# Handing the first tokens of the second layer over inside SBUF, with its weights loaded a stage earlier

## The chip, the cores and the metric

The kernel runs on one core of a Trainium2 chip. The metric is the device time of one execution in microseconds (us); the time given for a kernel is the median of its runs. The profile is one execution recorded by the hardware profiler, and all rows and lines quoted come from it. PE is the matrix engine, DVE the vector engine, ACT the scalar engine, POOL the general engine (GpSimd), and SP the engine that here only issues transfers (DMAs).

## The reference, cut to what matters

128 images of 128x128 pixels are turned into 64 tokens of 256 features each, by two convolutions. Two transformer layers follow.

```
h = tokenizer(x)                                    # (128, 64, 256)
h = h + relu_attention(layernorm(h))                # layer 0, within an image
h = h + expert_attention(layernorm(h))              # layer 0, 4 experts, residual inside
h = h + linear_attention(layernorm(h))              # layer 1, over the IMAGES, per token group
h = h + experts(layernorm(h))                       # layer 1, 8 experts, each token to one
```

What matters here is the border between the third and the fourth line. The attention of layer 0 works within one image, so its kernel keeps images on the partitions in pairs: partition `b*64 + t` holds token t of image b of the pair, and there are 64 pairs. The attention of layer 1 mixes over the 128 images for each token position, so it wants one image per partition, and tokens along the free axis. Between the two, h has to be turned round.

## The kernel before

All of h lives in SBUF as one tile, `c.h2`, [128, 64 pairs, 256], through the tokenizer and layer 0. Each stage is written in a hand-made order (`tc.manual_schedule()`): the order in the program is the order on each engine's queue, and only the semaphores that the framework derives from the data add waits.

**Expert attention** (`expert_attention`, L770 to L1318) loops over pairs p = 0 to 63. Iteration p works on three pairs at once: `new` (p+1: queries, keys, values), `cur` (p: scores, softmax) and `old` (p-1: transposed weights, `mixed`, `output`). The softmax of a pair comes in two halves x = 0 and 1: `less_max` on DVE (L1078, L1079), `exponents` on ACT (L1082), `sums` on DVE (L1085, L1086), `weights` on POOL (L1092, L1093: the gate into the reciprocal sums, then a product over 128x1024), `transposed` on PE with a copy by ACT (L1102, L1105). `mixed` (L1115, copy L1123) and `output` (L1129) end with `h2[:, p] += po` on DVE (L1130). In the last iteration, p = 63, there is no `new`, and after the loop pair 63 goes through `transposed`, `mixed` and `output` alone. After every fourth pair `output` writes four pairs, 512 KB, to a DRAM tensor `hd` of [image, token, feature] (L1132, on SP). This DRAM copy is what turns h round.

**Linear attention** (`linear_attention`, L1321 to L1788) works on 16 groups of four tokens. `Group.load` (L1370) reads hd[:, 4 tokens, :] (512 KB) into one of four buffers `x`; `statistics` on DVE (L1378, L1379, two instructions per token); `factors` on POOL (L1383 to L1386, four instructions per group); `normal` on ACT (L1389, one per token); `transpose` by PE with a copy by ACT (L1398, L1399). Then `queries_keys(i)` for each token (PE, L1426: four 128x512 matmul instructions each) with `queries_keys_kept` (DVE, L1430), `values` and so on, for four blocks of heads. Other steps are put at places of this loop by `at(n, i, step)`: block n, token i. The matmul results of `queries_keys` and `values` share a ring of three PSUM buffers (`psp`).

At the border everything is done in this order: pair 63 is added, the last four pairs are written to hd, the memory of h2 is released, new pools are opened, `Routing` loads a bias and a gate weight (SP) and makes its constants (POOL, one small PE product `wsum`, L1817), the weights `w`, `wvs`, `bs`, `bvs`, `wgs` are loaded on ACT's queue (L1340 to L1352), the groups 0 to 3 are loaded on SP's queue, and the statistics of groups 0, 1 and 2 begin:

```
            for g in range(4):
                groups[g].load()
            for g in range(3):
                for i in range(NG):
                    groups[g].statistics(i)
                groups[g].factors()
                if g == 0:
                    for i in range(NG):
                        groups[0].normal(i)
                    groups[0].transpose()
            groups[4].load()
```

`c.busy(out, x, n)` (L47) issues n matmuls of the identity with `x` whose result nobody reads.

Of the kernel before, what the change touches and what calls it, by code (L numbers as in the profile page):

```python
# [20 lines left out]
P = 128  # L21
B = 128
# [268 lines left out]
class Shared:  # L291
# [3 lines left out]
    def __init__(self, c, ctx):  # L295
        def pool(name, bufs, **k):
            return ctx.enter_context(c.tc.tile_pool(name=name, bufs=bufs, **k))

        self.np_, self.bp = pool("an", 2), pool("ab", 2)
        self.atp, self.ep, self.small = pool("aat", 1), pool("ae", 2), pool("as", 1)  # L300
        self.psq = pool("apq", 4, space=PSUM)
# [468 lines left out]
def expert_attention(c, sh, hd, normw, wr, br, wqkv, wvT, wproj, bproj, wout):  # L770
# [227 lines left out]
    class Pair:  # L998
# [89 lines left out]
        def weights(self, x):  # L1088

            e, sm = self.e[x], self.sm[x]  # L1090
            s2 = sm.rearrange("p (m e) -> p m e", e=2)
            nc.gpsimd.tensor_mul(s2, s2, bcast(self.blk.gate[:, self.n, x::2], 1, 8))  # L1092
            nc.gpsimd.tensor_mul(e, e, bcast(sm, 2, T))  # L1093
# [31 lines left out]
        def output(self):  # L1125
            p = self.p
            po = ps([P, D], "po")
            for fc in range(2):
                nc.tensor.matmul(po, self.z[:, fc], wt.o[:, fc, :], start=(fc == 0), stop=(fc == 1))  # L1129
            nc.vector.tensor_add(h2[:, p], h2[:, p], po)  # L1130
            if p % 4 == 3:
                nc.sync.dma_start(  # L1132
                    hd[2 * p - 6 : 2 * p + 2].rearrange("(n b) t f -> (b t) n f", b=2),
                    h2[:, p - 3 : p + 1],
                )

# [33 lines left out]
    def do(key):  # L1170
        for step in work.pop(key, ()):
            step()
# [46 lines left out]
    def first(cur, new, chunk, last):  # L1219

        new.queries_keys(0)
        chunk.exponents()
        new.queries_keys_copied(0)
        chunk.sums()
        chunk.weights()
        cur.scores()
        cur.less_max(0)
        y.normal_scalar(0)
        new.queries_keys(1)
        cur.less_max(1)  # L1230
        chunk.transpose()
        new.queries_keys_copied(1)
        chunk.transposed()
        cur.exponents(0)
        last.outcome(0)
        last.outcome(1)
        for par in range(2):
            last.outcome_copied(0, par)
        cur.sums(0)
        cur.weights(0)  # L1240
        cur.exponents(1)
        for par in range(2):
# [12 lines left out]
        new.values_kept(1)  # L1255
        last.back(2)
        last.back(3)
        last.added(2)
        last.added(3)
        for k in range(NB):  # L1260
            x.stream(k)
        do((0, "POOL"))
        do((0, "PE"))

    def rest(chunk, last):
        with (
# [6 lines left out]
            for p in range(NP):  # L1273
                new = Pair(p + 1, blocks[(p + 1) // NB]) if p + 1 < NP else None
                if p == 0:
                    first(cur, new, chunk, last)
                    old, cur = cur, new
                    continue
                do((p, "ACT"))
# [12 lines left out]
                cur.exponents(0)  # L1292
                if new:
                    new.queries_keys(1)
                    new.queries_keys_copied(1)
# [25 lines left out]
def linear_attention(c, hd, hx, out, k, wqk, bqk, wv, bv, wgb):  # L1321
# [7 lines left out]
    NG = 4  # L1329
    with (  # L1330
        tc.tile_pool(name="lw", bufs=1) as wp,
# [7 lines left out]
        w = wp.tile([P, 2, 2 * D], F32, name="w")  # L1339
        nc.scalar.dma_start(w, wqk.rearrange("(c p) n -> p c n", p=P))  # L1340
        wvs = wp.tile([P, 2, D], F32, name="wvs")
        nc.scalar.dma_start(wvs, wv.rearrange("(c p) n -> p c n", p=P))
        bs = wp.tile([P, 2 * D], F32, name="bs")
        nc.scalar.dma_start(bs, bqk.partition_broadcast(P))
        bvs = wp.tile([P, 32], F32, name="bvs")
        nc.scalar.dma_start(bvs, bv)

        wgs = wp.tile([P, 4, 32], F32, name="wgs")
        nc.gpsimd.memset(wgs, 0.0)
        for j in range(2):  # L1350
            r = slice(j * 64, j * 64 + 64)
            nc.scalar.dma_start(wgs[r, :, j * E : j * E + E], wgb.rearrange("(p f) e -> f p e", f=64))  # L1352
        ones = wp.tile([P, P], F32, name="ones")
        nc.gpsimd.memset(ones, 1.0)

        share = wp.tile([P, P], F32, name="share")
        nc.gpsimd.memset(share, 0.0)
        for hh in range(2):
            nc.gpsimd.memset(share[hh * 64 : hh * 64 + 64, hh * 64 : hh * 64 + 64], 1.0 / 64)

        class Group:
# [5 lines left out]
            def load(self):  # L1367
                g = self.g
                self.x = gp.tile([P, NG, D], F32, tag="x", name="x", bufs=4)
                nc.sync.dma_start(self.x, hd[:, g * NG : g * NG + NG, :])  # L1370

            def statistics(self, j):
                if j == 0:
                    self.mv = gp.tile([P, NG, 2], F32, tag="mv", name="mv", bufs=4)
                    self.rs = gp.tile([P, NG], F32, tag="rs", name="rs", bufs=4)
                    self.nb = gp.tile([P, NG], F32, tag="nb", name="nb", bufs=4)
                st = gp.tile([P, 6], F32, tag="st", name="st")
                nc.vector.bn_stats(st, self.x[:, j, :])  # L1378
                nc.vector.bn_aggr(self.mv[:, j, :], st)  # L1379

            def factors(self):
                mean, var = self.mv[:, :, 0], self.mv[:, :, 1]
                nc.gpsimd.tensor_scalar_add(self.rs, var, LN_EPS)  # L1383
                nc.gpsimd.tensor_tensor(self.rs, self.rs, c.nhalf[:, 0:NG], ALU.pow)
                nc.gpsimd.tensor_mul(self.nb, mean, self.rs)
                nc.gpsimd.tensor_sub(self.nb, c.zero[:, 0:NG], self.nb)  # L1386
# [250 lines left out]
        for n, x in enumerate(heads[:3]):  # L1637
# [52 lines left out]
        def last():  # L1690
# [55 lines left out]
            t = gp.tile([P, NG, D], F32, tag="x", name="dev", bufs=4)  # L1746
            routing.statistics(t, gp.tile([P, NG, D], F32, tag="x", name="var", bufs=4))
# [22 lines left out]
        with tc.manual_schedule():  # L1770
            for g in range(4):
                groups[g].load()
            for g in range(3):
                for i in range(NG):
                    groups[g].statistics(i)
                groups[g].factors()
                if g == 0:
                    for i in range(NG):
                        groups[0].normal(i)
                    groups[0].transpose()  # L1780
            groups[4].load()
            for n, x in enumerate(heads):
# [15 lines left out]
class Routing:  # L1798


    def __init__(self, c, gp, wg, bg):
# [5 lines left out]
        self.bgs = gp.tile([P, E], F32, name="bgs")  # L1807
        nc.sync.dma_start(self.bgs, bg.partition_broadcast(P))
        wgs = gp.tile([P, 2, E], F32, name="wgs")
        nc.sync.dma_start(wgs, wg.rearrange("(c p) e -> p c e", p=P))  # L1810
        self.ones = gp.tile([P, P], F32, name="ones")
        nc.gpsimd.memset(self.ones, 1.0)
        self.wsum = gp.tile([P, E], F32, name="wsum")
        with c.tc.tile_pool(name="gw", bufs=1, space=PSUM) as gpp:
            pw = gpp.tile([P, E], F32, name="pw")
            for fc in range(2):
                nc.tensor.matmul(pw, self.ones, wgs[:, fc, :], start=(fc == 0), stop=(fc == 1))  # L1817
            nc.vector.tensor_copy(self.wsum, pw)
# [13 lines left out]
        self.before = gp.tile([P, P], F32, name="before")  # L1832
# [4 lines left out]
        self.one = gp.tile([P, T], F32, name="one")  # L1837
        nc.vector.memset(self.one, 1.0)
        self.c = c
        self.mean, self.rs = (gp.tile([P, T], F32, name=n) for n in ("mean", "rs"))  # L1840
# [329 lines left out]
def vit_tower(ctx: ExitStack, tc: tile.TileContext, a, out):  # L2170
# [8 lines left out]
    with tc.tile_pool(name="stream", bufs=1) as sp:  # L2179
        c.h2 = sp.tile([P, B // 2, D], F32, name="h2")  # L2180
        tokenizer(c, a["x"], a["w1"], a["bn1"], a["w2"], a["bn2"])
        with ExitStack() as rings:
            sh = Shared(c, rings)
            beside, rest = expert_attention(
                c, sh, hd, *(a[k] for k in ("normw", "wr", "br", "wqkvf", "wvf", "wproj", "bproj", "wout"))
# [3 lines left out]
    with tc.tile_pool(name="gate", bufs=1) as gp:  # L2189
        k = Routing(c, gp, a["wg"], a["bg"])  # L2190
        linear_attention(c, hd, hx, out, k, a["wqk1"], a["bqk1"], a["wv1"], a["bv1"], a["wg"])
# [72 lines left out]
```

## Time and profile before

| | |
|---|---|
| time, median of 3 runs | 2685.99 us (2681.73 to 2687.66) |
| the profiled execution: time, span | 2687.57 us, 2685.8 us |
| mean granted TensorE clock | 0.981 |
| PE, DVE, ACT, POOL busy | 95%, 75%, 60%, 60% of the span |
| expert attention from 1108 us on, to 1883.4 us | PE busy 744.6 of 775.4 us |
| the border, 1883.4 to 1902.2 us | PE busy 3.6 of 18.8 us |
| linear attention, 1902.2 to 2202 us | PE busy 280.4 of 299.8 us |

How to read it: busy shares over the span mix stages with different limits, so the table's lower rows give the three stretches that the change touches. "Window" rows give, for a stretch of time, the busy time of PE, its weight loads, DVE, ACT and POOL with the number of instructions in brackets, then the mean clock granted to PE (1.00 is full speed, 0.50 half), the busy share of the DMA engines and GB/s. A "chain" row gives start, duration and what the end of the program was waiting for at that moment. A "timeline" row gives start and duration, engine, line, operation, output and inputs, and in brackets how long the engine stood idle before it and for whom.

### The profile page before, as it was taken

To read this page: it belongs to the slowest core of one execution; us is meant where nothing else is said; L and a number is where in the kernel's file an instruction comes from. 1 tells how busy PE (TensorE), PEld (TensorE's weight loads), DVE (VectorE), ACT (ScalarE), POOL (GpSimd) and SP (SyncE) were. 2 spreads that over 40 slices of the span, in tenths; PEclk is the share of its full clock that TensorE was granted. 3 is DMA by queue.
4 is the path that set the end of the run, shared out by engine and by line. 5 is a ranking of instruction groups with operands and counts; after the bars stand their busy time and mean duration, and the time that the engine had idled before them with its cause. 6 is when DMAs were issued, how large, how long until landed. Compare 5 with 4: busy or idle time off the path is not lost.

```text
span 2685.8 us, 80910 instructions
## 1 busy us (share of the span) xinstructions
PE 2539.0 (95%) x35229; PEld 1724.6 (64%) x35229; DVE 2024.2 (75%) x3028; ACT 1624.6 (60%) x3421; POOL 1618.6 (60%) x1381
## 2 busy tenths in 40 slices
PE   8989999999999999899999999999799987999997
PEld 4553444444444444688888888888466565888886
DVE  5759999999999989878877888877367786444443
ACT  2228888888888988766666666665245533332332
POOL 3318889888898998566666666653232312445544
PEclk9999999999999999999999999999899998999998
DMA  3100000000000000000000000000435454555554
GB/s 111 32 13 1 2 2 2 1 2 1 2 2 1 2 12 2 3 12 19 11 11 19 12 19 12 11 19 11 118 64 126 95 123 151 177 193 191 197 186 134
DMA packets 138271, 141.14 MB, mean 53 GB/s; under 512 B 107875, under 2 KB 121701, under 8 KB 130224
## 3 DMA queue, kind: packets, MB, share of 16 engines
q1 hardware_dynamic: 127536, 118.40, 14.8%
q0 software_dynamic: 7648, 14.77, 1.7%
q8 instruction: 278, 4.55, 0.7%
q10 hardware_dynamic: 2720, 2.69, 0.3%
q14 instruction: 89, 0.73, 0.1%
HBM read 104.03 MB, written 32.54 MB: 51 GB/s over the span
## 4 chain that ended last, share of the span: by engine, by line
PE 71%; DVE 18%; issue 4%; ACT 4%; POOL 1%; DMA 1%; DVEq 0%; POOLq 0%; SPq 0%; ACTq 0%
PE sc L340 12%; PE po L2108 6%; DVE m L530 6%; PE ph L2092 6%; PE pc L184 5%; PE pt L1102 4%; PE pqk L1019 4%; PE sc L1066 4%; PE pq L1426 4%; PE pv L1041 3%; PE pz L1115 3%; PE pt L587 2%; PE sc L525 2%; PE pv L1440 2%; PE pk L409 2%
## 5 line engine op out<-in xcount | busy, mean ns | idle before, releaser
L538 POOL TENSOR_TENSOR m<-q,k 128x1024 f32<-128x1024 f32 x384 | 720.1, 1906 | 69.3 <-PE sc L340 56.3
L530 DVE TENSOR_TENSOR m<-pc,k 128x2048 f32<-128x2048 f32 (+1 forms) x320 | 647.2, 2058 | 0.5 <-ACT q L474 0.5
L340 PE MATMUL sc<-m,wide 128*32 128x512 f32 x4096 | 517.3, 598 | 13.9 <-DVE m L530 7.9
L539 ACT ACTIVATE m<-m 128x1024 f32<-128x1024 f32 x384 | 403.0, 1050 | 11.1 <-POOL m L538 10.5
L340 PEld LDWEIGHTS sc<-m,wide 128*32 128x32 f32 x4096 | 127.8, 109 | 281.4 <-issue 165.7
L548 ACT ACTIVATE m<-k,q 128x64 f32<-128x64 f32 x1024 | 271.0, 340 | 0.9 <-DVE k L421 0.9
L1078 DVE TENSOR_REDUCE mx<-sc 128x16 f32<-128x1024 f32 x128 | 156.1, 1220 | 135.3 <-PE sc L1066 135.3
L1093 POOL TENSOR_TENSOR e<-e,mx 128x1024 f32<-128x1024 f32 x128 | 243.6, 1903 | 10.0
L1025 ACT COPY kr<-pqk 128x512 f32<-128x512 f32 x254 | 137.7, 603 | 140.4 <-PE pqk L1019 140.4
L2092 PE MATMUL ph<-xt,w1s 128*128 128x256 f32 x896 | 198.9, 380 | 3.6 <-DVE xt L2083 2.7
L2108 PE MATMUL po<-w2s,hT 128*128 128x256 f32 x896 | 198.0, 379 | 0.0
L1092 POOL TENSOR_TENSOR mx<-mx,gate 128x16 f32<-128x16 f32 x128 | 27.7, 216 | 278.9 <-ACT z L1123 152.7
L2092 PEld LDWEIGHTS ph<-xt,w1s 128*128 128x128 f32 x896 | 169.8, 190 | 28.3 <-DVE xt L2083 3.3
L2108 PEld LDWEIGHTS po<-w2s,hT 128*128 128x128 f32 x896 | 168.1, 190 | 21.7
L1105 ACT COPY pT<-pt 128x512 f32<-128x512 f32 x256 | 139.0, 598 | 50.4 <-PE pt L1102 50.0
L1079 DVE TENSOR_TENSOR e<-sc,mx 128x1024 f32<-128x1024 f32 x128 | 156.7, 1225 | 4.4
L2126 POOL DMA_INDIRECT out<-y,rout x56 | 56.8, 1013 | 167.7 <-ACT hT L2096 124.8
L1085 DVE TENSOR_REDUCE mx<-e 128x16 f32<-128x1024 f32 x128 | 152.5, 1191 | 4.0 <-ACT e L1082 3.8
L1102 PE MATMUL pt<-ident,e 128*128 128x128 f32 x1024 | 143.1, 282 | 9.5 <-DVE vr L1055 6.3
L2096 ACT ACTIVATE hT<-ph,w1s 128x256 f32<-128x256 f32 x224 | 93.2, 471 | 96.8 <-PE ph L2092 96.8
L2113 ACT ACTIVATE y<-y,gf 128x256 f32<-128x256 f32 x56 | 28.0, 507 | 196.4 <-issue 107.3
L1082 ACT ACTIVATE e<-e 128x1024 f32<-128x1024 f32 x128 | 139.5, 1090 | 2.2 <-DVE e L1079 1.9
(330 smaller groups left out, 5013.6 us busy)
## 6 DMA issues: line engine op xcount, KB each, us to landing
w1s<-in_we SPq DMA_DIRECT2D x30, 1028.0 KB, 5.2
w2s<-in_we SPq DMA_DIRECT2D x30, 1024.0 KB, 4.9
hd<-h SPq DMA_DIRECT2D x16, 512.0 KB, 3.4
x<-hd SPq DMA_DIRECT2D x16, 512.0 KB, 3.9
h<-hd SPq DMA_DIRECT2D x4, 2048.0 KB, 12.8
hx<-h SPq DMA_DIRECT2D x4, 2048.0 KB, 11.8
out<-h SPq DMA_DIRECT2D x4, 2048.0 KB, 20.6
xt<-in_x SPq DMA_DIRECT2D x15, 512.0 KB, 3.6
```

The source lines that it names most:

```text
L340: nc.tensor.matmul(dst[j : j + 32], wide[:, hf, s : s + 32], part, start=start, stop=stop)
L530: nc.vector.tensor_tensor(m, bcast(self.pq[:, hf, i : i + n], 3, T), k, ALU.max)
L538: nc.gpsimd.tensor_tensor(m, bcast(self.q[:, hf, s : s + 2], 3, T), k, ALU.subtract)
L539: nc.scalar.activation(m, m, AF.Relu)
L548: nc.scalar.activation(self.parts[i, hf][:, q], self.blk.k[:, hf, i], AF.Relu, bias=self.q[:, hf, i - NB // 2, q : q + 1], scale=-1.0,)
L1078: nc.vector.tensor_reduce(mx, sc, AX.X, ALU.max)
L1079: nc.vector.tensor_sub(e, sc, bcast(mx, 2, T))
L1085: nc.vector.tensor_reduce(self.sm[x], self.e[x], AX.X, ALU.add)
L1093: nc.gpsimd.tensor_mul(e, e, bcast(sm, 2, T))
L1102: nc.tensor.transpose(pt[:, cq, :], e[:, i : i + 2, :].rearrange("p e s -> p (e s)"), c.ident)
L2092: nc.tensor.matmul(ph[:, j], self.w1[:, w0 : w0 + P], self.xt[:, fc], start=(fc == 0), stop=(fc == 1))
L2108: nc.tensor.matmul(po, self.hT[:, f, r * P : r * P + P], self.w2[:, f, :], start=(f == 0), stop=(f == 7))
```

## The change

The second layer's weights and the first 16 tokens of every image (groups 0 to 3) are put into SBUF during the expert attention. For that, the tiles of the ReLU attention that are free after pair 0 are allocated on the other side of SBUF and released early, and a new class `Front` allocates there. At pair 8 it issues the weights' loads on SP and five memsets on POOL. At every fourth pair from p = 7 on it loads the rows of the eight images that were written four pairs earlier: 8 partitions of 16 KB. Pairs 60 and 61, pair 62 and pair 63 are written to hd on their own. Images 120 to 125 follow after pair 62; images 126 and 127 (pair 63) are copied from h2 to `x` within SBUF, one transfer for each image, before pair 63's write to hd.

In the last iteration `mixed` and `output` of pair 62 move up to just after `exponents(0)` of pair 63, three idle matmuls follow, and `weights(1)` of pair 63 goes to DVE. At the start of the linear attention seven idle matmuls are issued, the four group loads are gone, and group 0's factors and normalisation are done in two halves. Routing's loads move behind the load of group 4, its constants to block 0, token 9, and `wsum` to token 10.

```diff
     def output(self):
             nc.vector.tensor_add(h2[:, p], h2[:, p], po)
-            if p % 4 == 3:
+            if p == NP - 1:
+                front.rows(B - 2, B)
+            n = {NP - 3: 2, NP - 2: 1, NP - 1: 1}.get(p, 4 * (p % 4 == 3))
+            if n:
                 nc.sync.dma_start(
-                    hd[2 * p - 6 : 2 * p + 2].rearrange("(n b) t f -> (b t) n f", b=2),
-                    h2[:, p - 3 : p + 1],
+                    hd[2 * (p - n + 1) : 2 * p + 2].rearrange("(n b) t f -> (b t) n f", b=2),
+                    h2[:, p - n + 1 : p + 1],
                 )
+            if p == NP - 3:
+                front.rows(B - 16, B - 8)
+            elif p == NP - 2:
+                front.rows(B - 8, B - 2)
+            elif n == 4 and p > 3:
+                front.rows(2 * p - 14, 2 * p - 6)
...
+        sh.end.close()
+        front.open()
...
+                if p == 8:
+                    front.weights()
...
                 cur.exponents(0)
+                if not new:
+                    old.mixed()
+                    old.output()
+                    c.busy(ps([P, 2 * D], "idle"), wt.w, 3)
                 if new:
                     new.queries_keys(1)
                     new.queries_keys_copied(1)
                 cur.exponents(1)
...
-                cur.weights(1)
+                cur.weights(1, nc.gpsimd if new else nc.vector)
                 do((p, "POOL"))
-                old.mixed()
                 if new:
+                    old.mixed()
                     for h in range(2):
                         new.values(h)
                         new.values_kept(h)
-                old.output()
+                    old.output()
...
+class Front:
+    NG = 4
+    def open(self):
+        pool = self.c.tc.tile_pool
+        self.wp = self.ctx.enter_context(pool(name="lw", bufs=1, side="right"))
+        self.np_ = self.ctx.enter_context(pool(name="ln", bufs=4, side="right"))
+        self.x = self.wp.tile([P, 4, self.NG, D], F32, name="x")
+    def weights(self):
+        self.w = wp.tile([P, 2, 2 * D], F32, name="w")
+        nc.sync.dma_start(self.w, wqk.rearrange("(c p) n -> p c n", p=P))
...
+        self.wgs = wp.tile([P, 4, 32], F32, name="wgs")
+        nc.gpsimd.memset(self.wgs, 0.0)
...
+    def group(self, g):
+        return self.x[:, g % 4]
+    def rows(self, b0, b1):
+        n = 4 * NG
+        x = self.x.rearrange("p g t f -> p (g t) f")
+        if b1 < B:
+            nc.sync.dma_start(x[b0:b1], self.hd[b0:b1, 0:n, :])
+            return
+        for b in range(2):
+            nc.sync.dma_start(x[b0 + b : b0 + b + 1], self.c.h2[b * T : b * T + n, B // 2 - 1, :])
...
             def load(self):
-                self.x = gp.tile([P, NG, D], F32, tag="x", name="x", bufs=4)
+                self.x = front.group(g)
                 nc.sync.dma_start(self.x, hd[:, g * NG : g * NG + NG, :])
...
+        at(0, 9, routing.constants)
+        at(0, 10, lambda: routing.weights_sum(psp.tile([P, 2 * D], F32, tag="pp", name="pw")[:, 0:E]))
...
+            c.busy(psp.tile([P, 2 * D], F32, tag="pp", name="idle"), w[:, 0], 7)
             for g in range(4):
-                groups[g].load()
+                groups[g].x = front.group(g)
             for g in range(3):
                 for i in range(NG):
                     groups[g].statistics(i)
-                groups[g].factors()
+                    if g == 0 and i % 2:
+                        groups[0].factors(i - 1, i + 1)
+                        for j in range(i - 1, i + 1):
+                            groups[0].normal(j)
                 if g == 0:
-                    for i in range(NG):
-                        groups[0].normal(i)
                     groups[0].transpose()
+                else:
+                    groups[g].factors()
             groups[4].load()
+            routing.load()
```

More of the change, by code (lines that the diff above doesn't have):

```diff
@@ L291, with __init__, pool @@
 class Shared:
-    def __init__(self, c, ctx):
-        def pool(name, bufs, **k):
+    def __init__(self, c, ctx, end):
+        def pool(name, bufs, ctx=ctx, **k):
             return ctx.enter_context(c.tc.tile_pool(name=name, bufs=bufs, **k))
-        self.np_, self.bp = pool("an", 2), pool("ab", 2)
-        self.atp, self.ep, self.small = pool("aat", 1), pool("ae", 2), pool("as", 1)
+        self.np_, self.bp, self.small = pool("an", 2), pool("ab", 2), pool("as", 1)
+        self.atp, self.ep = (pool(n, k, end, side="right") for n, k in (("aat", 1), ("ae", 2)))
+        self.end = end
         self.psq = pool("apq", 4, space=PSUM)
@@ L767, in relu_attention, with expert_attention @@
     return old, blocks[-1]
-def expert_attention(c, sh, hd, normw, wr, br, wqkv, wvT, wproj, bproj, wout):
+def expert_attention(c, sh, front, hd, normw, wr, br, wqkv, wvT, wproj, bproj, wout):
     tc, nc, h2 = c.tc, c.nc, c.h2
@@ L1086, in sums, with weights @@
             nc.vector.reciprocal(self.sm[x], self.sm[x])
-        def weights(self, x):
+        def weights(self, x, eng=nc.gpsimd):
             e, sm = self.e[x], self.sm[x]
             s2 = sm.rearrange("p (m e) -> p m e", e=2)
-            nc.gpsimd.tensor_mul(s2, s2, bcast(self.blk.gate[:, self.n, x::2], 1, 8))
-            nc.gpsimd.tensor_mul(e, e, bcast(sm, 2, T))
+            eng.tensor_mul(s2, s2, bcast(self.blk.gate[:, self.n, x::2], 1, 8))
+            eng.tensor_mul(e, e, bcast(sm, 2, T))
         def transposed(self, x):
@@ L1318, in expert_attention, with __init__ @@
     return beside, rest
-def linear_attention(c, hd, hx, out, k, wqk, bqk, wv, bv, wgb):
+class Front:
+    NG = 4
+    def __init__(self, c, hd, wqk, bqk, wv, bv, wgb):
+        self.c, self.hd, self.inputs = c, hd, (wqk, bqk, wv, bv, wgb)
+        self.ctx = ExitStack()
+    def open(self):
[4 more added lines that the diff above has]
+    def weights(self):
+        c, nc, wp = self.c, self.c.nc, self.wp
+        wqk, bqk, wv, bv, wgb = self.inputs
+        self.w = wp.tile([P, 2, 2 * D], F32, name="w")
+        nc.sync.dma_start(self.w, wqk.rearrange("(c p) n -> p c n", p=P))
+        self.wvs = wp.tile([P, 2, D], F32, name="wvs")
+        nc.sync.dma_start(self.wvs, wv.rearrange("(c p) n -> p c n", p=P))
+        self.bs = wp.tile([P, 2 * D], F32, name="bs")
+        nc.sync.dma_start(self.bs, bqk.partition_broadcast(P))
+        self.bvs = wp.tile([P, 32], F32, name="bvs")
+        nc.sync.dma_start(self.bvs, bv)
+        self.wgs = wp.tile([P, 4, 32], F32, name="wgs")
+        nc.gpsimd.memset(self.wgs, 0.0)
+        for j in range(2):
+            r = slice(j * 64, j * 64 + 64)
+            nc.sync.dma_start(self.wgs[r, :, j * E : j * E + E], wgb.rearrange("(p f) e -> f p e", f=64))
+        self.ones = wp.tile([P, P], F32, name="ones")
+        nc.gpsimd.memset(self.ones, 1.0)
+        self.share = wp.tile([P, P], F32, name="share")
+        nc.gpsimd.memset(self.share, 0.0)
+        for hh in range(2):
+            nc.gpsimd.memset(self.share[hh * 64 : hh * 64 + 64, hh * 64 : hh * 64 + 64], 1.0 / 64)
+    def group(self, g):
+        return self.x[:, g % 4]
+    def rows(self, b0, b1):
+        nc, NG = self.c.nc, self.NG
+        n = 4 * NG
[5 more added lines that the diff above has]
+            nc.sync.dma_start(x[b0 + b : b0 + b + 1], self.c.h2[b * T : b * T + n, B // 2 - 1, :])
@@ L1327, in linear_attention @@
+def linear_attention(c, front, hd, hx, out, k):
     tc, nc = c.tc, c.nc
     lgs, sth, routing = k.lgs, k.sth, k
-    NG = 4
+    NG = front.NG
     with (
-        tc.tile_pool(name="lw", bufs=1) as wp,
         tc.tile_pool(name="lg", bufs=2) as gp,
@@ L1338, in linear_attention @@
     ):
[L1339 to L1359, printed above, removed]
+        w, wvs, bs, bvs, wgs = front.w, front.wvs, front.bs, front.bvs, front.wgs
+        ones, share = front.ones, front.share
         class Group:
@@ L1373, in statistics, with factors @@
                 if j == 0:
[L1374 to L1377, printed above, removed]
+                    self.mv = front.np_.tile([P, NG, 2], F32, tag="mv", name="mv")
+                    self.rs = front.np_.tile([P, NG], F32, tag="rs", name="rs")
+                    self.nb = front.np_.tile([P, NG], F32, tag="nb", name="nb")
+                st = front.np_.tile([P, 6], F32, tag="st", name="st")
                 nc.vector.bn_stats(st, self.x[:, j, :])
                 nc.vector.bn_aggr(self.mv[:, j, :], st)
[L1381 to L1386, printed above, removed]
+            def factors(self, i0=0, i1=NG):
+                i = slice(i0, i1)
+                mean, var, rs, nb = self.mv[:, i, 0], self.mv[:, i, 1], self.rs[:, i], self.nb[:, i]
+                nc.gpsimd.tensor_scalar_add(rs, var, LN_EPS)
+                nc.gpsimd.tensor_tensor(rs, rs, c.nhalf[:, i], ALU.pow)
+                nc.gpsimd.tensor_mul(nb, mean, rs)
+                nc.gpsimd.tensor_sub(nb, c.zero[:, i], nb)
             def normal(self, j):
@@ L1745, in last @@
             y.gates_added(1)
-            t = gp.tile([P, NG, D], F32, tag="x", name="dev", bufs=4)
-            routing.statistics(t, gp.tile([P, NG, D], F32, tag="x", name="var", bufs=4))
+            routing.statistics(front.group(0), front.group(1))
             x.gates(0)
@@ L1807, in __init__, with load, weights_sum, constants @@
         self.bgs = gp.tile([P, E], F32, name="bgs")
-        nc.sync.dma_start(self.bgs, bg.partition_broadcast(P))
-        wgs = gp.tile([P, 2, E], F32, name="wgs")
-        nc.sync.dma_start(wgs, wg.rearrange("(c p) e -> p c e", p=P))
-        self.ones = gp.tile([P, P], F32, name="ones")
-        nc.gpsimd.memset(self.ones, 1.0)
[L1813 to L1818, printed above, removed]
+        self.wgs = gp.tile([P, 2, E], F32, name="wgs")
+        self.ones = gp.tile([P, P], F32, name="ones")
+        self.wsum = gp.tile([P, E], F32, name="wsum")
+        self.before = gp.tile([P, P], F32, name="before")
+        self.one = gp.tile([P, T], F32, name="one")
+        self.c, self.gp, self.inputs = c, gp, (wg, bg)
+        self.mean, self.rs = (gp.tile([P, T], F32, name=n) for n in ("mean", "rs"))
+    def load(self):
+        nc, (wg, bg) = self.c.nc, self.inputs
+        nc.sync.dma_start(self.bgs, bg.partition_broadcast(P))
+        nc.sync.dma_start(self.wgs, wg.rearrange("(c p) e -> p c e", p=P))
+    def weights_sum(self, pw):
+        nc = self.c.nc
+        for fc in range(2):
+            nc.tensor.matmul(pw, self.ones, self.wgs[:, fc, :], start=(fc == 0), stop=(fc == 1))
+        nc.vector.tensor_copy(self.wsum, pw)
+    def constants(self):
+        nc, gp = self.c.nc, self.gp
+        nc.gpsimd.memset(self.ones, 1.0)
         def steps(name, pattern, shape, base=0, rows=0):
@@ L1831, in __init__ @@
         self.token = steps("token", [[1, T]], [P, T], base=1, rows=T)
-        self.before = gp.tile([P, P], F32, name="before")
         nc.gpsimd.memset(self.before, 1.0)
@@ L1836, in __init__ @@
         )
-        self.one = gp.tile([P, T], F32, name="one")
         nc.vector.memset(self.one, 1.0)
-        self.c = c
-        self.mean, self.rs = (gp.tile([P, T], F32, name=n) for n in ("mean", "rs"))
     def statistics(self, t, u):
@@ L2181, in vit_tower @@
         tokenizer(c, a["x"], a["w1"], a["bn1"], a["w2"], a["bn2"])
+        front = Front(c, hd, *(a[k] for k in ("wqk1", "bqk1", "wv1", "bv1", "wg")))
         with ExitStack() as rings:
-            sh = Shared(c, rings)
+            sh = Shared(c, rings, ExitStack())
             beside, rest = expert_attention(
-                c, sh, hd, *(a[k] for k in ("normw", "wr", "br", "wqkvf", "wvf", "wproj", "bproj", "wout"))
+                c, sh, front, hd, *(a[k] for k in ("normw", "wr", "br", "wqkvf", "wvf", "wproj", "bproj", "wout"))
             )
@@ L2190, in vit_tower @@
         k = Routing(c, gp, a["wg"], a["bg"])
-        linear_attention(c, hd, hx, out, k, a["wqk1"], a["bqk1"], a["wv1"], a["bv1"], a["wg"])
+        with front.ctx:
+            linear_attention(c, front, hd, hx, out, k)
         experts(c, hx, gfd, out, a["we1"], a["we2"], a["be2"], lambda: route(c, k, gfd))
```

## The prediction

> **What bounds the kernel now.** I read the page first, then cut the span into stretches with the windows view, then followed the chain of waits and the timeline across the border. Windows:
>
> ```profile
> 1883.40:1902.20 18.80, 3.61 (x13) 2.44 (x13) 6.81 (x28) 2.66 (x5) 6.41 (x23) 0.58 0.58 198
> 1902.20:1910.00 7.80, 7.80 (x19) 3.60 (x19) 3.62 (x9) 2.55 (x5) 0.92 (x5) 0.91 0.22 67
> 1910.00:1947.00 37.00, 36.76 (x139) 23.40 (x138) 15.57 (x39) 14.00 (x27) 6.37 (x15) 1.00 0.49 100
> ```
>
> PE is the limit on both sides of the border (36.8 of 37 us busy just after it) and works 3.6 us in the 18.8 us of the border itself. A microsecond taken from the border is a microsecond of span, since everything later hangs on PE's first `pq`. The chain says what fills it:
>
> ```profile
> 1882.95 0.43 DVE h L1130
> 1883.40 2.89 DMA hd<-h
> ...
> 1887.36 7.15 DMA x<-hd
> 1894.53 0.44 DVE st L1378
> ...
> 1898.88 0.61 ACT x L1389
> ...
> 1902.34 7.63 PE pq L1426 x16
> ```
>
> The last addition ends at 1883.37, the round trip through DRAM delays the first statistics to 1894.53 (11.16 us), and from there to the first `pq` (1902.16 in the timeline) it is 7.63 us. The last iteration of the expert attention, in the timeline:
>
> ```profile
> 1870.81 1.21 DVE L1085 TENSOR_REDUCE mx<-e 128x16 f32<-128x1024 f32 x1
> 1872.35 1.63 PE L1129 MATMUL po<-xTr,z 128*128 128x256 f32 x4 [2.53 <-ACT z L1123]
> 1872.67 1.90 POOL L1093 TENSOR_TENSOR e<-e,mx 128x1024 f32<-128x1024 f32 x1
> ...
> 1874.63 1.97 PE L1102 MATMUL pt<-ident,e 128*128 128x128 f32 x8 [0.65 <-POOL e L1093]
> 1874.83 1.90 POOL L1093 TENSOR_TENSOR e<-e,mx 128x1024 f32<-128x1024 f32 x1
> ```
>
> PE waits for POOL here, and runs slowly: the same 8 transposes take 1.09 us at 1863.36. The clock rows for it:
>
> ```profile
> 1868.00:1871.00 3.00, 1.74 (x52) 1.60 (x52) 2.97 (x4) 1.11 (x3) 0.00 (x0) 1.00 0.00 0
> 1874.00:1877.00 3.00, 2.18 (x9) 1.79 (x10) 0.42 (x1) 0.95 (x2) 2.65 (x3) 0.50 0.00 0
> ```
>
> **The change, part by part.** The sum is made against the profiled execution (span 2685.8, time 2687.57, so 1.8 us outside the span). The median of the runs is 1.6 us below that execution; I carry the difference over to the median.
>
> *Part 1, the round trip.* After the addition, SP issues two copies within SBUF, 0.36 us each by the row of L1132, so the second starts about 0.4 us after the addition. No row shows a copy into one partition. From below: the smallest loads land 1.7 to 1.9 us after issue (the DMA view's list of issues: `wr`, `wproj`, `wvf`). From above: 7.15 us, the crowded loads of the border. The queue is otherwise empty, so I take 2.5, towards the last hd write's 2.89 (512 KB against 16 KB each). First statistics at 0.03 + 0.37 + 2.5 + 0.05 = 2.95 us after the addition instead of 11.16: **-8.2** (-8.8 to -3.6). Gone with it are the loads of groups 0 to 3 and the weights, 198 GB/s in the border's row.
>
> What the moved transfers cost where they go: six loads at pair 8, sixteen row loads and two more hd writes, all on SP. In the expert attention SP has nothing else to issue (its wait for L1130 before the last write was 41.7 us), so an SP that waits blocks nobody until pair 63. The tightest: pair 62's hd write (about 1872) must land (2.9) before the rows of images 120 to 125 are issued (1875), which land by about 1878; the copies of pair 63 come at 1883. Five microseconds of cover; without it, up to 3 us. The pair-63 hd write now lands near 1887, and its first reader, group 4's load, is issued only after group 0's transposes (1892). The DMA engines were busy 0.05 of this stage, so transfers there cost nothing.
>
> [...]
>
> *Part 2, the start of the linear attention.* Statistics of two tokens end 1.17 us after the first starts (1894.53 to 1895.70); POOL starts 0.17 later and its four instructions take 1.92 (1896.93 to 1898.85); the second half follows on POOL: 1.17 + 0.17 + 1.92 + 0.07 + 1.92 = 5.25. Two `normal` end 1.07 later (6.32), then transposes and copy: before, `pq` began 1.21 after the last `normal` on a slow clock; on a fast one about 0.95. Total 7.27 against 7.63: **-0.4** (-0.6 to +0.6). Halving the factors gains only 0.1, since POOL pays its four instructions twice; the statistics of groups 1 and 2 stay behind PE's first 6.9 us of `pq`.
>
> *Part 3, the idle matmuls.* One fp32 128x512 product is two instructions in the trace (`pq` x4 for two products), 0.43 us each in the fast stretches. Seven are 6.0 us: from 1883 to 1889, just before the first `normal` ends (1889.3). Nothing needed is behind them unless PE is slow, when they take 12 us and would hold the transposes back by up to 2.5. What they buy: the first 16 `pq` took 7.81 us, fast ones 6.9: **-0.9** (0 to -0.9).
>
> *Part 4, the last iteration.* PE ends pair 62's `pz` at 1869.8; `z` now goes ahead of `exponents(1)`, so `po` runs 1870.3 to 1871.5 and the addition 1871.5 to 1871.95. On DVE this addition stands ahead of `sums(0)`, which ran at 1870.81: everything behind moves 1.16 us, and POOL's `weights(0)` ends at 1875.7 instead of 1874.57. `sums(1)` and its reciprocal end at 1874.85. Then `weights(1)` on DVE: 0.2 and 1.23 us by like rows, so 1876.3 if DVE is free. Here the trace has a row against it, DVE and POOL each multiplying 128x1024 with both inputs in SBUF:
>
> ```profile
> 2174.89 1.23 DVE L1549 TENSOR_TENSOR qk<-qk,ks 128x1024 f32<-128x1024 f32 x1
> 2175.00 2.88 POOL L1549 TENSOR_TENSOR qk<-qk,ks 128x1024 f32<-128x1024 f32 x1 [5.91 <-DVE ks L1544]
> ```
>
> POOL's usual 1.90 became 2.88: it waited for DVE to end. [...] POOL starts first here, so DVE waits until 1875.73 and ends at 1877.2. [...] PE: half 0 from 1875.8 to 1876.9, half 1 from 1877.25 to 1878.35, last copy 1879.15, `pz` to 1880.9 (52 instructions in 1.74 after such a copy at 1868.08), `z`, `po`, addition to 1883.05, against 1883.37: **-0.3** if the clock holds. The three idle matmuls (2.6 us, 1871.5 to 1874.1) leave a gap of 1.7. If it drops as before, the transposes cost 0.88 each and `pz` 0.5 more: +1.2. Range -0.7 to +1.2.
>
> *Part 5, what moves into covered places.* `wsum` at token 10: four small matmuls with their weight loads, 0.99 slow, about 0.5 fast, in a stretch where PE is full: **+0.5** (0.3 to 1.0, with one more tile in the PSUM ring). Routing's constants (2 us) at token 9 fall into POOL's idle 11 us before L1383: 0. Five memsets at pair 8, 0.9 us on POOL, come when POOL had 0.6 us to spare before L1092: **+0.2** (0 to 0.4).
>
> Sum: -8.2 - 0.4 - 0.9 - 0.3 + 0.5 + 0.2 = **-9.1**. Span 2676.7, median 2685.99 - 9.1 = 2676.9; I write 2677. A measurement of this kernel can tell about 0.2% (5.4 us) from no change.
>
> **The rivals.** *The clock stays low* (0.16). For: a pause of 2.5 us at 1869.8 was enough to halve it, and group 0's transposes come in two clumps 2 us apart. Against: the idle matmuls. Without part 3, part 4 at +1.2 and part 2 at 0: -6.3, 2679.7. *The copies land late* (0.13): one partition takes 16 KB, and both copies end on neighbouring partitions; at 7 us instead of 2.5 the gain is -4.6, 2681.4. Against: 16 KB is 1/32 of what took 7.15. *It doesn't do what it says* (0.03): the first statistics still wait for pair 63's write to hd. That lands 0.8 us after the copies, so -8.3: no separate number. *Slower* (0.04): the four groups' buffers become one tile; if waits covered the whole tile, each of the 11 later loads would hold the next statistics until it lands, 3.9 us, of which PE's ring hides about one token, 1.7: 11 x 2.2 = 24, less 9: +15, 2701. It decides from 0.8 us exposed for each load. Against: h2 is also one tile, written slice by slice beside its hd writes, and L1130 waits for nothing but PE there.
>
> **How the numbers follow.** The forecast has 0.64, 2677. The bounds of parts 1 to 5, the late copies and the scatter of the runs (6 us over three) give 2671 to 2682. Faster by over 0.2% needs 5.4 of the 9.1: nearly all of the forecast, four fifths of the low clock, a third of the late copies: 0.85. Within 0.2%: 0.11. Slower: 0.04.
>
> **What would show it.** Right: no `x<-hd` among the chain's pieces at the border; first L1378 row (new number) some 3 us after the last addition, first `pq` some 10 us after it; the stretch between them at a clock above 0.9; the border 9 us shorter and all later stretches as long as before. [...] Wrong: a DVE wait for `x` inside the linear attention, a PE wait before the transposes on the idle matmuls, or an iteration at pairs 8 to 60 longer than before.

## The result, and the profile after

| | before | changed |
|---|---|---|
| time, median of 6 runs each | 2685.89 us (2681.73 to 2687.66) | 2674.6 us (2671.17 to 2677.69) |
| ratio, 95% interval | | 0.9962 [0.9949, 0.9974] |
| the profiled execution: time, span | 2687.57, 2685.8 us | 2677.69, 2675.9 us |
| the same ratio, a second time (8 and 16 runs) | | 0.9970 [0.9958, 0.9983] |

The change makes the kernel faster by 0.3 to 0.4%, about 11 us in the first comparison and 7 us in the second. Executions of one kernel lie 6 to 10 us apart in these two comparisons, and up to 15 us in the experiments, so single microseconds are read from the profiles, as intervals between two events at the border. The last column is the profile of the changed kernel that was taken in the second comparison; there is one profile of before.

| interval (us) | before | changed | difference | changed, repeat |
|---|---|---|---|---|
| start of pair 63's scores to the end of the last addition ("the last iteration") | 18.99 | 18.19 | -0.80 | 18.65 |
| last addition to the first statistics | 11.16 | 3.02 | -8.14 | 3.02 |
| first statistics to the first `pq` | 7.63 | 6.61 | -1.02 | 6.60 |
| first `pq` to the fourth token kept (start of the fourth L1430, now L1488) | 7.85 | 8.69 | +0.84 | 8.73 |
| sum | 45.63 | 36.51 | -9.12 | 37.00 |

The profile of the changed kernel gives no chain of waits across the border, so the border is read from the timeline (the bracket is how long the engine stood idle, and for whom):

```profile
1881.35 0.42 DVE L1132 TENSOR_TENSOR h<-h,po 128x256 f32<-128x256 f32 x1 [5.36 <-PE po L1131]
1881.80 1.25 SPq L1395 DMA_DIRECT2D x<-h  x2
1881.83 6.28 PE L50 MATMUL idle<-w,ident 128*128 128x512 f32 x14 [0.51 <-DVE h L1132]
1883.09 0.59 SPq L1138 DMA_DIRECT2D hd<-h  x1
...
1884.79 0.43 DVE L1435 BATCH_NORM_STATS2 st<-x 128x6 f32<-128x256 f32 x1 [3.02 <-DMA x<-h]
...
1886.39 0.72 POOL L1442 TENSOR_TENSOR rs<-rs,nhalf 128x2 f32<-128x2 f32 x1
...
1891.40 8.65 PE L1484 MATMUL pq<-w,xT 128*128 128x512 f32 x16 [0.24 <-ACT xT L1457]
```

The last addition ends at 1881.77, the two copies are issued at once, and the first statistics start at 1884.79, released by the copies (`x<-h`), no longer by a load from DRAM. The 14 instructions of the seven idle matmuls fill PE's pause to 1888.1. The windows that answer to the three of before (PE, weight loads, DVE, ACT, POOL busy; clock; DMA share; GB/s):

```profile
1881.77:1891.40 9.63, 8.02 (x23) 3.52 (x23) 6.20 (x26) 2.82 (x6) 4.42 (x13) 0.98 0.05 17
1891.40:1900.05 8.65, 8.65 (x18) 3.90 (x19) 3.96 (x11) 2.40 (x5) 1.87 (x6) 0.82 0.23 62
1900.05:1937.05 37.00, 36.76 (x141) 23.45 (x140) 15.34 (x40) 13.53 (x26) 7.68 (x23) 1.00 0.48 100
```

The border's 18.8 us are 9.63 now, its DMA traffic has gone from 198 to 17 GB/s, and its clock from 0.58 to 0.98. The second row has the surprise: the first 16 `pq` run at a mean clock of 0.82, below the 0.91 of before, and take 8.65 us (before 7.81). From there on PE is as full as it was: 36.76 of 37 us.

### The profile page after: what moved, and what is told of

Its sections match the earlier page's. It is cut to its first block, busy times and chain, and to the rows that moved or that the text cites. A ratio compares the mean times of both kernels' runs of the same rounds, so it can differ in the third digit from the quotient of the medians.

```text
span 2675.9 us, 80960 instructions
## 1 busy us (share of the span) xinstructions
PE 2543.2 (95%) x35249; PEld 1724.9 (64%) x35249; DVE 2026.1 (76%) x3030; ACT 1624.4 (61%) x3421; POOL 1617.8 (60%) x1383
```

## The experiments

All are edits of the changed kernel. But for two single executions their medians lie between 2672 and 2680 us, most with overlapping intervals, so the readings rest on the border's intervals, each from one profile. "Addition to statistics" means from the end of the last addition to the first statistics of group 0.

**Where the 8.1 us come from: groups 0 to 3 loaded from DRAM again, the weights still early.**

```diff
-            if p == NP - 1:
-                front.rows(B - 2, B)
...
-            if p == NP - 3:
-                front.rows(B - 16, B - 8)
...
-                groups[g].x = front.group(g)
+                groups[g].load()
```

> The changed kernel, but no row is loaded early and nothing is passed within SBUF: groups 0 to 3 are loaded from hd at the border again. Weights, idle matmuls, last iteration and Routing's places stay changed. Theory (the round trip was the gain): last addition to first statistics goes from 3.02 us to about 7 to 8 (2.9 for the write to land, about 0.5, 4 for the load), so 4 to 5 us slower than the changed kernel, about 2679. It would be the full 11.2 of before only if the crowding by the weights were not part of it. Rival (the gain is mainly the weights' early load and the last iteration): the interval grows by under 2 us and the time stays within 2 us of 2674.6.

Measured: 2676.56 us, ratio 0.9973 [0.9964, 0.9981]. The timeline:

```profile
1877.51 0.42 DVE L1132 TENSOR_TENSOR h<-h,po 128x256 f32<-128x256 f32 x1 [5.36 <-PE po L1131]
1877.96 0.33 SPq L1136 DMA_DIRECT2D hd<-h  x1
...
1879.72 1.74 SPq L1419 DMA_DIRECT2D x<-hd  x4
...
1883.74 0.43 DVE L1427 BATCH_NORM_STATS2 st<-x 128x6 f32<-128x256 f32 x1 [5.80 <-DMA x<-hd]
```

Addition to statistics is 5.81 us with the whole round trip in place, less than the 7 to 8 expected, where before it was 11.16. So 5.35 of the 8.14 us do not belong to the round trip as such. Piece by piece: the write, now of one pair (128 KB) instead of four, is done after 1.76 us (1877.96 to 1879.72; before 2.89); the load follows at once (before 1.07 later, behind the release of h2's memory and Routing's two loads); and it lands in 4.02 us (before 7.15). That is 1.13 + 1.07 + 3.13 = 5.33.

**The last pair through DRAM, all other images early.**

```diff
-            if p == NP - 1:
-                front.rows(B - 2, B)
...
+            if p == NP - 1:
+                nc.sync.dma_start(
+                    front.x.rearrange("p g t f -> p (g t) f")[B - 2 : B], hd[B - 2 : B, 0 : 4 * front.NG, :]
+                )
```

> The changed kernel, but images 126 and 127 go through hd like all others (one load of two rows after their write has landed) in place of the two copies within SBUF. Theory: last addition to first statistics becomes a write's landing (2.9 us for 512 KB before, some 2 to 2.5 for 128 KB), 0.5 and a small load's landing (about 2): 5 to 5.5 us in place of 3.02, so 2 to 2.5 us slower than the changed kernel, about 2677. Rival (the write to hd lands as soon as a copy, and the wait of the statistics is for that write anyway): no difference, 3 to 3.5 us.

Measured: 2679.07 us, ratio 0.9984 [0.9977, 0.9991].

```profile
1879.11 0.42 DVE L1132 TENSOR_TENSOR h<-h,po 128x256 f32<-128x256 f32 x1 [5.36 <-PE po L1131]
1879.56 0.34 SPq L1136 DMA_DIRECT2D hd<-h  x1
...
1881.28 0.24 SPq L1142 DMA_DIRECT2D x<-hd  x1
...
1883.79 0.43 DVE L1437 BATCH_NORM_STATS2 st<-x 128x6 f32<-128x256 f32 x1 [4.25 <-DMA x<-hd]
```

4.26 us (5 to 5.5 were expected): a write of 1.72 and a load of 2.51. The ladder is now whole: 11.16 (before), 5.81 (nothing heavy around the round trip), 4.26 (only 32 KB on the way back), 3.02 (no DRAM). The copy within SBUF, the most striking part of the change, is worth 1.24 us.

**Do the weights' loads explain the 7.15 us landing?** Four kernels tried to put these loads back to the border on ACT's queue, two with the groups' loads late as well, two with them early. All four have this (and idle matmuls of the identity with itself, since `w` is late), and then differ in where the call stands (ahead of the second layer's code, or, in the last two, inside its hand-made order):

```diff
-                if p == 8:
-                    front.weights()
...
-        nc.sync.dma_start(self.w, wqk.rearrange("(c p) n -> p c n", p=P))
+        nc.scalar.dma_start(self.w, wqk.rearrange("(c p) n -> p c n", p=P))
...
+        front.weights()
```

Both ahead of the order:

> The changed kernel with the groups' loads and the weights' loads both back at the border, the weights on ACT's queue as before (the seven idle matmuls are replaced by 28 of 128 columns, which need no weight). With only the groups at the border, last addition to first statistics had been 5.81 us. Theory (most of the 11.16 us of before was crowding: five weight loads and four group loads at once): the interval returns to about 9 us, 3 more than with the groups alone. Rival (the weights land beside them for nothing): it stays near 5.8 us.

> The changed kernel with the weights' loads alone back at the border on ACT's queue (28 idle matmuls of 128 columns in place of the seven of 512), the rows loaded early. Theory (the weights matter only by crowding the rows; alone they land within 5 to 9 us, before the first pq needs them 9.6 us after the last addition): last addition to first statistics 3.0 to 3.6 us and last addition to first pq within 0.5 us of 9.6. Rival (the weights themselves were what the border waited for): first pq 1.5 us later or more.

Both inside it, one execution each:

> As e5, but with the weights' loads written inside the hand-made order of the linear attention, on ACT's queue, so that they are issued at the border and not when the memory comes free (in e5 they went out at about 1113 us, far ahead). Groups 0 to 3 are loaded at the border too. Theory (crowding): last addition to first statistics 7.5 to 9.5 us, in place of 5.8 with the groups alone; before, the group's load took 7.15 us to land against about 3.9 alone. Rival (the landing of before had another reason, such as SP's two small loads ahead of it): 5.8 to 6.5.

> As e6, but with the weights' loads at the border inside the hand-made order, on ACT's queue; the rows early and the copies within SBUF as changed. Theory: ACT issues them ahead of the last addition, they take about 5 us and are in place before pq (9.6 us after the addition); [...] last addition to first statistics 3.0 to 4.5 us, first pq at most 1.5 us later. Rival (the weights were what mattered): first pq more than 3 us later.

Addition to statistics was 5.82 and 5.85 us with the groups late, 3.02 and 3.02 with them early; the times were 2677.43 (ratio 0.9973 [0.9962, 0.9985]) and 2675.11 us (0.9973 [0.9962, 0.9985]), and 2682.19 and 2684.05 in the single executions. That looks like "the weights don't matter", and it would be a wrong reading. The tile view of the weights says when they were issued, first in the third of these kernels, then in the kernel before:

```profile
L1352 ACTq DMA_DIRECT2D w<-in_wqk x1: 378/378/378, 1110.2 to 1110.2; - x1
...
DMA to landing us min/median/max: 4.0/4.0/4.0
```

```profile
L1340 ACTq DMA_DIRECT2D w<-in_wqk x1: 406/406/406, 1886.4 to 1886.4; - x1
...
DMA to landing us min/median/max: 5.3/5.3/5.3
```

They went out at 1110 us (at 1109 to 1114 in all four), as soon as their memory was free, more than 750 us ahead of the border; before, they had to wait for h2's memory. None of the four tested the crowding. What speaks for it is the traffic while the first group's load was on its way, before and in the first experiment:

```profile
1887.36:1894.51 7.15, 0.99 (x4) 0.93 (x4) 0.17 (x1) 0.00 (x0) 1.12 (x8) 0.50 0.82 281
1879.72:1883.74 4.02, 4.02 (x11) 1.71 (x9) 0.00 (x1) 0.00 (x0) 0.00 (x0) 1.00 0.73 218
```

281 GB/s over 7.15 us are 2.01 MB, 218 over 4.02 are 0.88 MB. The difference, 1.13 MB, is about what the six weight loads of before move (512, 256, 256, 16 and twice 8 KB, 1.08 MB). The weights' own landing times say less: `w` took 5.3 us at the border of before against 4.0 above, and `bs` 7.9 against 4.2, but in the changed kernel, at pair 8, they took 4.8 and 6.0. So that the 3.13 us went to the weights' loads is likely, and no experiment shows it.

**Without the ten idle matmuls.**

```diff
-                    c.busy(ps([P, 2 * D], "idle"), wt.w, 3)
...
-            c.busy(psp.tile([P, 2 * D], F32, tag="pp", name="idle"), w[:, 0], 7)
```

> The changed kernel without its three and seven idle matmuls. Theory (they keep PE's clock up): granted clock falls to 0.5 in the last iteration, its two times 8 transposes take 1.97 us in place of 1.09, last scores to last addition 19.5 us or more in place of 18.2; the first pq after the border take 8 us or more for 16; in all 1.5 to 3 us slower than the changed kernel. Rival (they hold the clock in neither place, as the 8.65 us for the 16 pq in the profile suggests): last scores to last addition within 0.3 us of 18.2 and the time the same.

Measured: 2677.4 us, ratio 0.9977 [0.9968, 0.9987]. The last iteration's interval is 20.20 us instead of 18.19. Its timeline and two windows:

```profile
1874.04 3.67 PE L1104 MATMUL pt<-ident,e 128*128 128x128 f32 x16 [4.21 <-POOL e L1095]
...
1877.64 3.13 PE L1117 MATMUL pz<-pT,vr 128*64 128x64 f32 x64
```

```profile
1871.00:1874.00 3.00, 0.00 (x0) 0.00 (x0) 2.90 (x5) 0.00 (x0) 2.12 (x2) 0.84 0.24 76
1874.00:1877.00 3.00, 2.96 (x14) 2.96 (x15) 1.24 (x2) 1.22 (x3) 0.00 (x0) 0.50 0.00 0
```

PE waits 4.21 us with nothing to do, the clock is halved, and the 16 transposes take 3.67 us where the changed kernel needs twice 1.09. The three idle matmuls there are worth 2.0 us against this profile of the changed kernel, and 1.7 against the mean of eight profiles with its last iteration (below). The seven at the border are worth 0.7 us here: statistics to first `pq` 6.75 against 6.61, and the first 16 `pq` 9.24 us against 8.65.

**The last softmax half on POOL again.**

```diff
-                cur.weights(1, nc.gpsimd if new else nc.vector)
+                cur.weights(1)
```

> The changed kernel with pair 63's weights(1) left on POOL. The DVE product stood 0.7 us behind POOL in the changed kernel (its first, 128x16 one took 0.90 us in place of 0.2). Theory [...]: POOL ends half 1 at 1.90 + 0.3 us after half 0, DVE did at 1.29 after it, so last scores to last addition grows by 0.8 to 0.9 us, to 19.0. Rival (the copies by ACT hide which engine does it): it stays within 0.3 us of 18.2.

Measured: 2677.66 us, ratio 0.9979 [0.9969, 0.9989]; the last iteration takes 20.59 us, 2.4 more than in the changed kernel.

```profile
1873.22 1.09 PE L1104 MATMUL pt<-ident,e 128*128 128x128 f32 x8 [1.63 <-POOL e L1095]
...
1875.38 1.97 PE L1104 MATMUL pt<-ident,e 128*128 128x128 f32 x8 [1.07 <-POOL e L1095]
```

The second half's transposes start 2.16 us after the first's (1.29 in the changed kernel): 0.9 us. The rest is the clock (0.57 from 1875 to 1878 us): PE's pause before them grows from 0.20 to 1.07 us, and the eight instructions that took 1.09 take 1.97. In this profile DVE's help is worth more through the clock than by its own speed; the expectation, 0.8 to 0.9 us, had only the latter.

**The old order of the last iteration altogether.**

```diff
-                if not new:
-                    old.mixed()
-                    old.output()
-                    c.busy(ps([P, 2 * D], "idle"), wt.w, 3)
...
-                cur.weights(1, nc.gpsimd if new else nc.vector)
+                cur.weights(1)
                 do((p, "POOL"))
+                old.mixed()
...
+                old.output()
```

> The changed kernel with the last iteration in the old order: mixed and output of pair 62 at its end, weights(1) on POOL, no three idle matmuls. Theory: last scores to last addition returns to the 18.99 us of before, 0.8 us more than the changed kernel, with a low clock in it. Rival (the reorder gained nothing, since the addition of pair 62 now holds sums(0) back): 18.2 us or less.

Measured: 2675.74 us, ratio 0.9971 [0.9962, 0.998]; the interval is 18.82 us, as before's 18.99. Eight profiles with the change's own last iteration (the changed kernel, its repeat, and the runs with late rows, a late last pair or moved weights) have 18.19 to 18.93, on average 18.5. So the three edits together are worth 0.3 to 0.5 us, but two of them without the third cost 1.4 to 1.8 us more than the old order, in one profile each: the new order makes a pause that the idle matmuls and DVE must fill.

**A better order: the first half's sums ahead of pair 62's addition, and the second copy issued on ACT's queue.**

```diff
                     old.mixed()
+                    cur.sums(0)
                     old.output()
...
-            nc.sync.dma_start(x[b0 + b : b0 + b + 1], ...)
+            (nc.sync, nc.scalar)[b].dma_start(x[b0 + b : b0 + b + 1], ...)
```

> The changed kernel with two orders mended: on DVE sums(0) of pair 63 stands ahead of pair 62's addition, and the copy of image 127 goes on ACT's queue, so that it doesn't wait for SP's first issue (0.63 us each in the profile). Theory: last scores to last addition 0.8 to 1.0 us shorter than 18.19 (17.2 to 17.4), last addition to first statistics 0.4 to 0.6 us shorter than 3.02. Rival (the end of the iteration is set by ACT's copies or PE, and the copies land together anyway): both within 0.2 us of the changed kernel. In the time, 1.4 us is too little to tell from no change.

Measured: 2671.97 us, ratio 0.9966 [0.9952, 0.9979].

```profile
1866.53 1.21 DVE L1087 TENSOR_REDUCE mx<-e 128x16 f32<-128x1024 f32 x1
...
1868.40 1.90 POOL L1095 TENSOR_TENSOR e<-e,mx 128x1024 f32<-128x1024 f32 x1
...
1869.75 0.58 DVE L1094 TENSOR_TENSOR mx<-mx,gate 128x16 f32<-128x16 f32 x1
...
1877.40 0.61 SPq L1397 DMA_DIRECT2D x<-h  x1
1877.40 0.60 ACTq L1397 DMA_DIRECT2D x<-h  x1
```

The last iteration falls from 18.19 to 17.27 us: as expected, since pair 62's addition no longer holds up the sums that POOL waits for. The two queues issue the copies at the same moment and gain nothing, where 0.4 to 0.6 us were expected: 2.98 us from the addition instead of 3.02. The 0.9 us can't be told from no change in the times.

**The same, with two idle matmul instructions between group 0's transposes.**

```diff
+                        if fill and fc == 0 and j == 1:
+                            c.busy(psp.tile([P, 2 * D], F32, tag="pp", name="idle"), w[:, 0], fill)
...
-                    groups[0].transpose()
+                    groups[0].transpose(1)
```

> f8 with one idle product of 512 columns between the first two and the last transposes of group 0's first half, where PE stands 0.74 us idle, to keep the clock for the first pq. Theory [...]: the first 16 pq take 6.9 us in place of 8.65 (changed) or 7.13 (f8), at the price of 0.1 us before the first pq. Rival [...]: 16 pq somewhere from 7 to 9.5 us again, as over the other kernels. Either way within 2 us of f8 in time.

Measured: 2678.66 us, ratio 0.9975 [0.9965, 0.9986]. The first 16 `pq` take 7.13 us, but they do so without the filling in the run above too. Inconclusive: what decides whether the clock drops here was set in neither run (last section).

**The changed kernel again.**

> The changed kernel unaltered, to stand beside f11 on the same chip and for a second look at its intervals: last scores to last addition 18.2 us, last addition to first statistics 3.0, first statistics to first pq 6.6; the first 16 pq anywhere from 7 to 9.5 us[...]. About 0.4% faster than before.

Measured: 2678.05 us, ratio 0.9970 [0.9958, 0.9983]; intervals 18.65, 3.02, 6.60 and 8.73 us. The copies' 3.02 and the start's 6.6 us repeat to 0.01 us, the last iteration to half a microsecond, and the slow first `pq` (8.69 us) are there again.

## Why the prediction was right, step by step

The median that was forecast, 2677, lies 2.4 us above the first median and 1.1 below the second. The terms are near as well, but part of that is luck. Parts 1 to 4, the border, add up to -9.8 in the forecast and to -9.12 in the profile (-8.63 in the repeat), with errors in them that cancel; of part 5, +0.7, outside the border, +0.42 is seen. That makes -8.7 against -9.1. The two profiles are 9.92 us apart at the fourth token, since the changed one was 0.80 us ahead already when pair 63's scores began.

- *Part 1, -8.2: right in size (-8.14), half right in content.* The first statistics came as estimated (2.95 us, measured 3.02), though two errors cancel in it: issuing a copy took 0.6 us, not 0.36, and a copy landed 2.2 us after its issue (median of the DMA view), not 2.5. But the sum took the whole 11.16 us for the price of a round trip through DRAM; it is 5.81 us when only one pair is written, the load follows at once and the weights are gone. These three together were worth 5.35 us, the early rows 1.55, the copy within SBUF 1.24. The row loads cost nothing, as estimated: the first statistics wait for `x<-h` alone.
- *Part 2, -0.4: measured -1.02.* The mis-sized step is "POOL pays its four instructions twice": the row L1442 took 0.72 us for 128x2 where it takes 1.03 for 128x4, so a half costs less than a whole. The four instructions of a half take 1.6 us (1886.06 to 1887.66), not 1.92, twice; that is the 0.6 us.
- *Part 3, -0.9: wrong, +0.84.* The step that failed is "What they buy": seven idle matmuls end at 1888.1, and `pq` begins at 1891.4. In these 3.3 us PE does only two clumps of transposes, the clock was taken down at their end, and the first 3.1 us of `pq` ran at half speed:

```profile
1884.30:1887.70 3.40, 3.40 (x9) 1.33 (x7) 2.74 (x11) 0.01 (x1) 1.40 (x5) 1.00 0.08 27
1887.70:1891.10 3.40, 2.09 (x9) 0.94 (x8) 3.16 (x14) 2.51 (x5) 2.92 (x8) 1.00 0.00 0
1891.10:1894.50 3.40, 3.16 (x5) 1.50 (x5) 0.64 (x3) 2.70 (x6) 1.71 (x5) 0.50 0.59 157
```

The stretch of 3.4 us in which PE works 2.09 us is followed by a whole one at 0.50. So the rival "the clock stays low" came true in part: not before the first `pq`, where the clock is 0.98, but in it. It cost 1.7 us against the forecast of this part (+0.84 instead of -0.9); the rival had 2.8 us over three parts.

- *Part 4, -0.3: -0.80 in this profile, -0.34 in the repeat, -0.5 on average of the eight.* The clock held, as assumed, and the order of events is the one written down: DVE waits for POOL.

```profile
1872.80 1.90 POOL L1095 TENSOR_TENSOR e<-e,mx 128x1024 f32<-128x1024 f32 x1
...
1873.83 0.90 DVE L1094 TENSOR_TENSOR mx<-mx,gate 128x16 f32<-128x16 f32 x1
...
1874.77 1.22 DVE L1095 TENSOR_TENSOR e<-e,mx 128x1024 f32<-128x1024 f32 x1
```

POOL's product ends at 1874.70; DVE's little product of 128x16, which takes POOL itself 0.22, takes 0.90 here and ends at 1874.73, and the large one starts only then. With the sums first it takes 0.58 and ends at 1870.33, again 0.03 us after POOL's product (1870.30). So in both profiles DVE was done with it only when POOL was, one instruction earlier than the prediction looked for a wait: the large product ran at its usual 1.22. That DVE would wait at all was the author's estimate from the one row of before (2.88 us beside DVE's 1.23). The forecast's figure for a dropped clock doesn't add up: -0.3, twice 0.88 and 0.5 make +2.0, not +1.2. The two runs in which the clock did drop took 1.2 and 1.6 us more than before (20.20 and 20.59).

- *Part 5, +0.5 and +0.2: +0.42, and not told.* Up to token 9 of block 0 every `queries_keys_kept` comes 9.92 us earlier than before. At token 10, where `wsum`'s four products (1918.9 to 1919.9) stand in PE's full queue, that falls to 9.50, and it stays at 9.47 to 9.50 for 30 tokens. The memsets' 0.2 us are lost in the expert attention, in which the lead of the changed profile wanders between -0.3 and 3.6 us.

The rival that ended slower (waits on the whole tile, 11 times 2.2 us) is refuted: in the linear attention no statistics wait for `x`, and PE is busy 36.76 of 37 us there.

## What to carry to other kernels

Before moving data another way than through DRAM, look at how large the last write is, what stands ahead of the load on its queue, and what lands beside it. Here that was two thirds of the 8.1 us (the share of what lands beside it, 3.1 us, is argued from bytes), and the copy within SBUF less than a sixth. Where PE pauses for some microseconds at a stage's border, plan the pause up to the first useful matmul; here the filling ended 3.3 us ahead of it, and the first products ran slow in most profiles (8.1 to 9.5 us for the first 16, against 7.1); what a filling up to it gains is not shown. And when an experiment moves a transfer, look up its issue time before reading the result.

## What the hardware showed that was not expected

- The same sequence can get either clock. From the first `pq` to the fourth token kept it took 7.2 us in four of the changed kernels' profiles and 8.2 to 9.5 in the others. In the profiles of before and of the changed kernel, all changes of the granted clock between 1500 and 2250 us lie a whole number of 3.413 us apart, to within 0.03 us (in the changed kernel at 1891.08, 1894.48, 2034.44 and 2037.84, say). This grid lies differently against the work: its last point ahead of the first `pq` comes 0.3 us before it in the changed kernel, and 2.0 us in the kernel before. The changed kernel and the one with the sums first do the same work from the addition to the first `pq` in 9.63 and 9.57 us. In the former, PE works 2.09 of the 3.4 us ahead of the half speed, shown above. In the latter it works less, 1.95 of the 3.44 us ahead of the first `pq`, and full speed stays:

```profile
1883.50:1886.94 3.44, 1.95 (x9) 0.94 (x8) 3.23 (x14) 2.56 (x6) 2.82 (x8) 1.00 0.00 0
1886.94:1890.30 3.36, 3.36 (x8) 1.63 (x9) 1.57 (x5) 2.40 (x5) 1.62 (x4) 1.00 0.57 160
```

The other profiles with this sequence differ as well: in the repeat, the old order and POOL's weights the first 16 `pq` took 8.69, 8.47 and 8.83 us, in the two with early groups and moved weights, whose idle matmuls last 6.52 instead of 6.28 us, 7.13. In the four runs whose first statistics came later, PE paused for 1.5 to 3.0 us between the idle matmuls and the transposes, and the 16 took 8.1 to 9.5 us. PE's work between two points of the grid does not decide alone: in the changed kernel, stretches with 1.76 and 1.99 us of it (from 1703.35 and 1955.93 us) were followed by full speed, and stretches with 2.50 and 2.53 (from 2126.60 and 2136.84 us) by half speed. What decides is not shown; no run set on purpose where the pause falls.

- POOL's power (`pow`, L1442) costs 0.72 us for 128x2 and 1.03 for 128x4: by an estimate from these two rows, some 0.4 us fixed and 0.16 for each column.
- Two copies of 16 KB, issued one after the other on one queue (1.25 us of issue for both) or at once on two, were both there about 3 us after the addition (3.02 and 2.98).
